# Giving the matmuls of a gathered row tile in one block: layers 2 and 3 of a graph attention kernel

## The chip, the cores and the metric

The kernel runs on one core of a Trainium2 chip. The metric is the device time of one execution in microseconds; the time given for a kernel is the median of several executions. Beside the times there is one execution with a profile, which shows the work of each engine: PE (matmuls) with PEld (its weight loads), DVE, ACT and POOL (elementwise work; POOL here issues the indirect gathers), and SP, which issues plain DMAs.

## The reference

Four graph attention layers over N = 4096 nodes with 256 features and one adjacency matrix, of which about 0.4% of the entries (and the diagonal) are set. Each layer is wrapped in a residual and a layer norm:

```python
x = _layernorm(x + _L0_gnn_ref(x, adj, ...))   # 4 heads of 64
x = _layernorm(x + _L1_gnn_ref(x, adj, ...))   # 4 heads of 64
x = _layernorm(x + _L2_gnn_ref(x, adj, ...))   # 2 heads of 128
x = _layernorm(x + _L3_gnn_ref(x, adj, ...))   # softmax and negative softmax, fc, elu
```

Layers 2 and 3, which the change touches, come down to this:

```python
# layer 2: two heads
e = leaky_relu(s1[:, None, :] + s2[None, :, :], 0.2)
att = softmax(where(adj[:, :, None] == 1, e, NEG), axis=1)
h_prime = einsum('ijh,jhc->ihc', att, W3h)

# layer 3: one logit, two softmaxes over the same neighbours
e = leaky_relu(Wh1 + Wh2.T, 0.2)
attention = softmax(where(adj > 0, e, NEG_INF), axis=1)
negative_attention = -softmax(where(adj > 0, -e, NEG_INF), axis=1)
h_prime_double = concatenate([attention @ x, negative_attention @ x], axis=1)
return elu(h_prime_double @ fc_W)
```

## The kernel before, in words

The 4096 nodes are 32 tiles of 128 rows. Since the adjacency is sparse, most tiles of a layer are *gathered*: for the 128 target rows of a tile the value rows of their neighbours are fetched by indirect DMA into slots of 128 rows, weights are worked out for each slot, and matmuls with the weights as the stationary operand and the fetched rows as the moving one sum them up. A bit mask per slot says which target row each fetched row belongs to.

A row tile has two halves of seven slots. A slot is used in one of two ways. A *full* slot has a 128x128 weight tile and gives one matmul. A slot of a *pair* holds neighbours of only 64 of the target rows; it has a 128x64 weight tile, and the two slots of a pair write to the two halves of the output's partitions. Half 0 has the tile's own rows as its full slot (fetched by a plain DMA that SP issues in `load`, line 797) and three pairs, so six gathers; half 1 has two pairs and three full slots, so seven gathers. `FULL` and `PAIRS` (lines 80 and 81) list the places; `parts` (line 807) gives each its slots. The gathers are issued by POOL at line 802.

For each half, `half` (line 840) makes the mask (`unpack`), then the weights `w`: in layer 2 by exponentials on ACT (line 912) and a masking step on DVE (line 914), in layer 3 by ACT at lines 879, 880 and 882 and by DVE at 881 and 883. Behind these stand the matmuls (line 933), once for each of the two heads (layer 2) or of the two softmaxes (layer 3). In layer 2 the row has 2 x 129 columns and both heads share a bank; in layer 3 each softmax has 257 columns and a bank of its own. Each matmul in the source gives two records in the profile.

The order of the matmuls at line 933 in layers 2 and 3 is set by the loop over `turns`. With F for full and P for pairs, and the heads in turn, layer 2 gives F P, P F in half 0 and F P, P F in half 1; layer 3 gives F P, F P in half 0 and F P, P F in half 1. The last half of the last tile of layer 3 has a function of its own, `last_half`, which gives each place as soon as its weights are there.

Some tiles are not gathered but *whole*: `whole_rows` (line 1173) goes through all 32 column tiles for four or three target tiles at once. It fetches values (`vw`, through SP's queue, four ahead), makes dense weights (`pw`, ACT and DVE, lines 1205 and 1206 in layer 2, 1208 to 1213 in layer 3) and multiplies (line 1216). Layer 2 has 11 whole and 21 gathered tiles, layer 3 seven and 25. This work is cut into units, and `whole` gives some of them after each half, so that they spread evenly over the gathered tiles.

`steps` runs `part(m, 0)` and `part(m, 1)` for each gathered tile, and `half_with_whole` gives, for each part, this order of work: loads and gathers of tiles `m` and `m + 1` (in part 0), the transposes of a projection for the next layer if one is ready (line 682), the half itself, the copy of the transposed tile (`xT`, ACT, line 687) and the projection's matmuls (line 696), the end of the tile before, units of whole tiles, and the projection's values. A projection is the matmul of a finished row tile with the next layer's weights; layer 3 has none. At a layer's end, `close` gives half 0 of the next layer's tiles 0 and 1 ahead of time.

This is an order of priority; a scheduler in the framework moves instructions on each engine where that lets them start sooner, and puts in the waits. Each engine then works in its own fixed order.

Buffers come from pools. `wp` has five buffers for `w`, each half taking one. `g0` and `g1` have four slots each for the gathered rows of half 0 and half 1; a slot holds all seven rows of a half in layer 2, and four of them in layer 3 (`PER`), where a half thus takes two slots. `ld` has four buffers for the target rows' logits, `vp` six for `vw` and `dp` eight for `pw`. A buffer comes free with the last instruction that reads it, so a gather waits until the matmuls of an earlier tile have read its slot.

Of the kernel before, what the change touches and what calls it, by code (L numbers as in the profile page):

```python
# [50 lines left out]
P = 128  # L51
# [27 lines left out]
UNITS = (1 + FIRST, NPACK - FIRST)  # L79
FULL = ((0,), tuple(range(NPAIR - FIRST, NPACK - FIRST)))  # L80
PAIRS = (tuple(range(1, 1 + FIRST)), tuple(range(NPAIR - FIRST)))
# [8 lines left out]
HEADS = (4, 4, 2, 2)  # L90
WIDTH = (65, 65, 129, 257)
# [670 lines left out]
class RowTile:  # L762
# [3 lines left out]
    def __init__(self, layer, step, m):  # L766
        self.layer, self.step, self.m = layer, step, m
        self.slots = {}
        self.accs = None

    def slot(self, half, s):
        L, n = self.layer, self.layer.n
# [64 lines left out]
        u, k = FULL[half][0], 0 if own else two  # L837
        spread(L.nc, words[:, u:u + len(FULL[half]), :], bits[:, k:k + len(FULL[half])], pat)

    def half(self, half):  # L840
        L, n, nc = self.layer, self.layer.n, self.layer.nc
        prog, sh, S = L.prog, L.shared, self.S
        H, Wd, V, T, A = HEADS[n], WIDTH[n], VALS[n], TERMS[n], LOGS[n]
        if self.accs is None:
            pool = prog.ptwo[1 if n == 3 and self.step % 2 else 0]
            self.accs = [prog.bank(pool) for _ in range(2 if n == 3 else 1)]
        accs, U = self.accs, UNITS[half]
        parts = self.parts(half)
        if n < 2:

# [4 lines left out]
            mh = there.bitcast(U8)  # L855
            mh2 = mh.rearrange("p (o i) -> p o i", o=1).to_broadcast([P, 2, U * P])
        else:
            there = prog.mkp.tile([P, UNITS[1], P // 4], I32, name="mk")[:, :U]
            self.unpack(half, there)
            mh = there.rearrange("p t i -> p (t i)").bitcast(U8).rearrange("p (t i) -> p t i", t=U)  # L860
        pairs = [prog.wp.tile([P, 2, UNITS[1], P], F32, name="w") for _ in range(H // 2)]
        w = [pair[:, k, :U] for pair in pairs for k in range(2)]
        if n < 2:
            w = [w[1], w[2], w[3], w[0]]
# [8 lines left out]

        if n == 3:
            if half == 1 and self.step == L.count - 1:
                return self.last_half(accs, parts, w, mh)
            for u in range(U):
                for rows, g in parts[u]:
                    nc.scalar.activation(w[0][:, u, rows], S[:, 0, rows], AF.Relu, bias=d(g, 0))  # L879
# [1 line left out]
            nc.vector.tensor_tensor(w[1], w[1], mh, op=ALU.mult)  # L881
            self.exps = nc.scalar.activation(w[0], w[0], AF.Exp, bias=sh["shift2"])
            nc.vector.tensor_tensor(w[0], w[0], mh, op=ALU.mult)
            turns = ((1,), (0,))
        else:
            for h in range(A, T):
                dd = self.slot(half, 0)[:, :HALF * ROW[n]].rearrange("p (t c) -> p t c", t=HALF)
                k = 0
                for us in sorted((PAIRS[half], FULL[half])):
                    two = us == PAIRS[half]  # L890
                    a, b = us[0], us[-1] + 1
                    e = (2 if two else 1) * (b - a)
                    rows = P // (e // (b - a))
# [23 lines left out]
            if n == 0:  # L917
                with self.layer.prog.tc.issue_after(last.ins):
                    nc.vector.tensor_scalar(self.kept(half), self.came(half), 0, None, op0=ALU.bitwise_or)
            turns = ((3, 0), (1, 2)) if n < 2 else ((0,), (1,))  # L920


        for t, heads in enumerate(turns):
            for us in (FULL[half], PAIRS[half])[::-1 if t == 1 and (half == 1 or n < 3) else 1]:
                for h in heads:
                    for u in us:
                        for rows, g in parts[u]:
                            a = accs[h][rows, :Wd] if n == 3 else accs[0][rows, h * Wd:(h + 1) * Wd]
                            b = g[:, h * Wd:(h + 1) * Wd]
                            if n < 2:  # L930
                                a = accs[0][rows, h * Wd:(H + 1) * Wd].rearrange("p (s c) -> p s c", c=Wd)[:, ::H - h]
                                b = b.rearrange("p (s c) -> p s c", s=1).to_broadcast([P, 2, Wd])
                            nc.tensor.matmul(a, w[h][:, u, rows], b,  # L933
                                             start=half == 0 and u == 0 and (n == 3 or h == turns[0][0]),
                                             stop=half == 1, skip_group_check=True)

    def last_half(self, accs, parts, w, mh):

# [21 lines left out]
class Layer:  # L960
# [62 lines left out]
    def half_alone(self, m, part):  # L1023


        self.step = 2 * m + part
        proj, middle = None, self.middle
        second = m > NT - (LATE if self.n == 0 else 6) and len(self.ready) > 1
        if self.ready and self.ready[0][0] < self.step and (part == 0 or second):
            self.set_banks()  # L1030
            if part == 1 and self.n == 0:
                self.prog.banks = self.prog.pplace
            proj = Projection(self.prog, self.n + 1, self.nxt, *self.ready.pop(0)[1:])
            proj.transpose()
        if part == 1 or self.tile(m).accs is None:
            self.tile(m).half(part)
        for p in self.stored:
            p.store()
        if proj is not None:
            proj.copy()  # L1040
        if proj is not None:
            proj.multiply()
        if middle is not None:
            middle.values()
        if part == 1 and m >= 1:
            self.tile(m - 1).finish()
        if middle is not None:
            middle.edge()
        self.stored, self.middle = [middle] if middle is not None else [], proj

    def half_with_whole(self, m, part):
# [12 lines left out]
        with ExitStack() as order:  # L1064
            for ins in self.last:
                order.enter_context(self.prog.tc.issue_after(ins))
            self.last = ()
            if part == 1 or self.tile(m).accs is None:
                self.tile(m).half(part)
                if self.outs:  # L1070


                    order.enter_context(self.prog.tc.issue_after(self.tile(m).exps.ins))
                    self.store_rows()
# [777 lines left out]
```

## Time and profile before

| | us |
|---|---|
| time, median of 3 executions (2794.93 to 2804.66) | 2798.34 |
| the profiled execution, its own time | 2791.46 |
| span of the profile | 2789.7 |
| PE busy | 2102.6 |
| DVE busy | 1550.7 |
| ACT busy | 1508.9 |
| POOL busy | 1392.2 |
| gathers on POOL (line 802), 1378 | 1386.9 |
| gathered matmuls (line 933), 9268 records, all layers | 1164.6 |
| whole-tile matmuls (line 1216), 2304 records | 415.1 |
| projections (line 696), 640 records | 214.1 |

The span is the time from the first to the last instruction of the profiled execution. Busy times of PE count a pipelined matmul with its modelled end, so the mean of one record is longer than the distance from one record's start to the next. Layer 2 runs from about 1770 to 2250 us in the span, layer 3 from about 2274 on.

### The profile page before, as it was taken

What the parts mean: (1) busy time and instruction counts of PE and PEld (TensorE: products, weight loads), DVE (VectorE), ACT (ScalarE), POOL (GpSimd) and SP (SyncE); (2) the same over time, 40 slices, a digit from 0 to 9 for tenths busy, and PEclk for the clock granted to TensorE, in tenths of its full rate; (3) what the DMA queues carried; (4) which work ended last, traced back from release to release, by engine and by line L of the source; (5) the groups of instructions that cost most, each with busy time, mean ns of one, the idle gap of its engine ahead of it and who ended that gap; (6) DMA issues with size and microseconds to landing.
All of it is one profiled execution on the core that took longest, in us unless ns stands there. A gap on an engine that the chain in (4) does not pass through costs nothing.

```text
span 2789.7 us, 46645 instructions
## 1 busy us (share of the span) xinstructions
PE 2102.6 (75%) x15137; PEld 1662.9 (60%) x15137; DVE 1550.7 (56%) x5130; ACT 1508.9 (54%) x4705; POOL 1392.2 (50%) x1413
## 2 busy tenths in 40 slices
PE   5546677667676675688787888768888889988886
PEld 3335555455455564567666676657877766765654
DVE  3335545455454355556565656647756656666565
ACT  5446455455454354444454545456756647766663
POOL 0254534434435444555555553456656446666663
PEclk7667777677676688788888888879989999999988
DMA  8767565555553344344444444335556567878774
GB/s 278 249 202 222 163 176 164 163 163 175 156 148 111 86 121 137 109 134 125 127 122 128 124 118 120 110 107 162 166 147 172 150 190 226 243 240 249 241 231 129
DMA packets 294057, 459.20 MB, mean 165 GB/s; under 512 B 90982, under 2 KB 206795, under 8 KB 293804
## 3 DMA queue, kind: packets, MB, share of 16 engines
q0 software_dynamic: 76544, 233.01, 29.2%
q1 hardware_dynamic: 212642, 218.92, 26.2%
q10 hardware_dynamic: 4618, 4.20, 0.4%
q8 instruction: 122, 2.00, 0.3%
q14 instruction: 131, 1.07, 0.1%
HBM read 407.14 MB, written 48.81 MB: 163 GB/s over the span
## 4 chain that ended last, share of the span: by engine, by line
PE 49%; issue 13%; ACT 4%; POOL 3%; DMA 2%; DVE 2%; another core or an unknown queue 1%; SPq 0%; ACTq 0%; POOLq 0%; DVEq 0%
PE bank L933 26%; PE bank L1216 12%; PE bank L696 4%; ACT w L912 3%; POOL G L802 3%; PE bank L1279 2%; PE bank L1277 2%; DMA G<-vals,idx 1%; PE bank L682 1%; PE bank L699 1%; DVE w L869 0%; ACT pw L1205 0%; PE bank L527 0%; PE bank L529 0%
## 5 line engine op out<-in xcount | busy, mean ns | idle before, releaser
L802 POOL DMA_INDIRECT G<-vals,idx x1378 | 1386.9, 1006 | 1365.2 <-issue 651.9
L933 PE MATMUL bank<-G,w 128*64 128x130 f32 (+5 forms) x9268 | 1164.6, 329 | 393.7 <-issue 357.6
L933 PEld LDWEIGHTS bank<-G,w 128*64 128x64 f32 (+1 forms) x9268 | 895.4, 173 | 632.1 <-issue 526.3
L912 ACT ACTIVATE w<-S,G 128x64 f32<-128x64 f32 (+1 forms) x3108 | 827.1, 350 | 104.5 <-issue 24.8
L1216 PE MATMUL bank<-vw,pw 128*128 128x129 f32 (+1 forms) x2304 | 415.1, 333 | 77.1 <-issue 72.8
L1216 PEld LDWEIGHTS bank<-vw,pw 128*128 128x128 f32 x2304 | 357.5, 203 | 130.2 <-issue 100.6
L869 DVE SCALAR_TENSOR_TENSOR w<-w,bank 128x1024 f32<-128x1024 f32 (+1 forms) x240 | 322.8, 1345 | 116.9 <-ACT w L912 103.0
L696 PE MATMUL bank<-wext,xT 128*128 128x268 f32 (+3 forms) x640 | 214.1, 472 | 38.8 <-ACT xT L687 24.5
L716 ACT ACTIVATE row<-bank 128x4 f32<-128x4 f32 (+1 forms) x128 | 21.6, 169 | 322.2 <-remote 106.6
L1205 ACT ACTIVATE pw<-Sw,d 128x512 f32<-128x512 f32 (+1 forms) x192 | 128.3, 679 | 119.9 <-remote 58.7
L1206 DVE SCALAR_TENSOR_TENSOR pw<-pw,mw 128x512 f32<-128x512 f32 (+1 forms) x192 | 122.1, 643 | 114.8 <-ACT pw L1205 86.6
L696 PEld LDWEIGHTS bank<-wext,xT 128*128 128x128 f32 x640 | 135.7, 231 | 74.8 <-ACT xT L687 27.9
L879 ACT ACTIVATE w<-S,G 128x64 f32<-128x64 f32 (+1 forms) x343 | 111.3, 354 | 101.3 <-DMA G<-vals,idx 58.4
L687 ACT COPY xT<-bank 128x256 f32<-128x256 f32 x128 | 46.3, 364 | 210.2 <-PE bank L682 132.8
L718 DVE COPY row<-bank 128x6 f32<-128x6 f32 (+2 forms) x128 | 20.0, 156 | 229.9 <-ACT row L716 202.3
L404 ACT ACTIVATE mk<-raw 128x1024 uint8<-128x1024 int32 x128 | 129.1, 1049 | 18.2 <-DMA raw<-in_adjB_dram 8.3
L1279 PE MATMUL bank<-pw,vw 128*65 128x128 f32 x512 | 115.7, 313 | 2.5 <-issue 2.4
L1213 DVE TENSOR_TENSOR pw<-pw,mw 128x512 f32<-128x512 f32 (+1 forms) x128 | 79.1, 621 | 68.7 <-ACT w L879 12.4
L1277 PE MATMUL bank<-vw,pw 128*128 128x65 f32 x512 | 102.9, 288 | 15.9 <-issue 15.7
L1277 PEld LDWEIGHTS bank<-vw,pw 128*128 128x128 f32 x512 | 94.5, 230 | 28.3 <-issue 26.9
L747 ACT ACTIVATE erow<-bank,shift 4x128 f32<-4x128 f32 (+1 forms) x96 | 33.5, 352 | 130.9 <-PE bank L737 77.9
L515 DVE TENSOR_TENSOR under<-bank,ranks 128x512 f16<-128x512 f32 x32 | 21.9, 685 | 139.9 <-remote 68.4
(197 smaller groups left out, 2179.6 us busy)
## 6 DMA issues: line engine op xcount, KB each, us to landing
raw<-in_adjB_dram SPq DMA_DIRECT2D x128, 512.0 KB
G<-vals,idx POOLq DMA_INDIRECT x1378
vw<-vals SPq DMA_DIRECT2D x128, 128.5 KB
S<-edge SPq DMA_DIRECT2D x60, 256.0 KB
vw<-vals SPq DMA_DIRECT2D x96, 129.0 KB
xp<-y SPq DMA_DIRECT2D x96, 128.0 KB
y<-xp SPq DMA_DIRECT2D x96, 128.0 KB
vals<-row SPq DMA_DIRECT2D x64, 152.0 KB
```

What stands on the lines that cost most here:

```text
L404: nc.scalar.activation(self.mk[:, 2 * q:2 * q + 2], src, AF.Copy)
L696: nc.tensor.matmul(pp[:, :c1 - c0], self.xT[:, k, :], wext[:, k, c0:c1], start=(k == 0), stop=(k == KT - 1 and brow is None))
L802: nc.gpsimd.indirect_dma_start(out=self.row(half, k), out_offset=None, in_=self.values[:N + 1 if half else MIX * P, :].rearrange("r (k c) ...
L869: return nc.vector.scalar_tensor_tensor(pair, pair, LEAST, mh2, op0=ALU.max, op1=ALU.mult)
L879: nc.scalar.activation(w[0][:, u, rows], S[:, 0, rows], AF.Relu, bias=d(g, 0))
L912: nc.scalar.activation(w[h][:, u, rows], S[:, h, rows], AF.Exp, bias=d(g, h))
L933: nc.tensor.matmul(a, w[h][:, u, rows], b, start=half == 0 and u == 0 and (n == 3 or h == turns[0][0]), stop=half == 1, skip_group_check=True)
L1205: nc.scalar.activation(p, S[:, h, :g], AF.Exp, bias=d)
L1206: nc.vector.scalar_tensor_tensor(p, p, LEAST, mj, op0=ALU.max, op1=ALU.mult)
L1216: nc.tensor.matmul(accs[it][:, c:c + Wd], p[:, it, :], v[:, c:c + Wd], start=(j == 0 and h == heads[0]), stop=(j == NT - 1), skip_group_ch ...
L1277: nc.tensor.matmul(bu[:, it * Wd:(it + 1) * Wd], p[up][:, it, :], v[:, up * Wd:(up + 1) * Wd], start=j == 0 and it == 0, **how)
L1279: nc.tensor.matmul(bf[:Wd, it * P:(it + 1) * P], v[:, flat * Wd:(flat + 1) * Wd], p[flat][:, it, :], start=j == 0 and it == 0, **how)
```

## The change

In layers 2 and 3, `half` for part 0 makes its mask and weights as before but gives no matmuls: it puts the half on a list (`held`). Part 1 makes its own weights, and then `multiply_held` gives the matmuls of both halves in one block: the full slot of half 0 (the tile's own rows), the pairs of half 0, the pairs of half 1, and the full slots of half 1, each for both heads or softmaxes. The output banks are taken at the first matmul. Layers 0 and 1 keep their order of matmuls, through the same new function `multiply`. The halves that `close` gives ahead of time are not held. In the last half of layer 3's last tile the held half is given in front of `last_half`.

```diff
-    def half(self, half):
+    def half(self, half, hold=False):
+        self.begun = True
...
-        if self.accs is None:
-            pool = prog.ptwo[1 if n == 3 and self.step % 2 else 0]
-            self.accs = [prog.bank(pool) for _ in range(2 if n == 3 else 1)]
-        accs, U = self.accs, UNITS[half]
+        U = UNITS[half]
...
             if half == 1 and self.step == L.count - 1:
-                return self.last_half(accs, parts, w, mh)
+                self.multiply_held()
+                return self.last_half(self.accs, parts, w, mh)
...
-            turns = ((1,), (0,))
...
-            turns = ((3, 0), (1, 2)) if n < 2 else ((0,), (1,))
-        for t, heads in enumerate(turns):
-            for us in (FULL[half], PAIRS[half])[::-1 if t == 1 and (half == 1 or n < 3) else 1]:
-                for h in heads:
-                    for u in us:
-                        for rows, g in parts[u]:
...
-                            nc.tensor.matmul(a, w[h][:, u, rows], b,
-                                             start=half == 0 and u == 0 and (n == 3 or h == turns[0][0]),
-                                             stop=half == 1, skip_group_check=True)
+            turns = ((0,), (1,)) if n == 2 else ((0, 1), (2, 3)) if A == T else ((3, 0), (1, 2))
+        if n < 2:
+            for t, heads in enumerate(turns):
+                for us in (FULL[half], PAIRS[half])[::-1 if t == 1 else 1]:
+                    for h in heads:
+                        self.multiply(half, h, us, parts, w, h == turns[0][0])
+            return
+        self.held.append((half, parts, w))
+        if not hold:
+            self.multiply_held()
+
+    def multiply(self, half, h, us, parts, w, first):
+        n = self.layer.n
+        H, Wd = HEADS[n], WIDTH[n]
+        if self.accs is None:
+            pool = self.layer.prog.ptwo[1 if n == 3 and self.step % 2 else 0]
+            self.accs = [self.layer.prog.bank(pool) for _ in range(2 if n == 3 else 1)]
+        accs = self.accs
+        for u in us:
+            for rows, g in parts[u]:
+                a = accs[h][rows, :Wd] if n == 3 else accs[0][rows, h * Wd:(h + 1) * Wd]
+                b = g[:, h * Wd:(h + 1) * Wd]
...
+                self.layer.nc.tensor.matmul(a, w[h][:, u, rows], b, start=half == 0 and u == 0 and first,
+                                            stop=half == 1, skip_group_check=True)
+
+    def multiply_held(self):
+
+        n, held = self.layer.n, self.held
+        heads = (0, 1) if n == 2 else (1, 0)
+        for group in (FULL, PAIRS):
+            for half, parts, w in held:
+                if half == 0:
+                    for h in heads:
+                        self.multiply(half, h, group[half], parts, w, n == 3 or h == heads[0])
+        for group in (PAIRS, FULL):
+            for half, parts, w in held:
+                if half == 1:
+                    for h in heads:
+                        self.multiply(half, h, group[half], parts, w, False)
+        self.held = []
...
-            if part == 1 or self.tile(m).accs is None:
-                self.tile(m).half(part)
+            if part == 1 or not self.tile(m).begun:
+                self.tile(m).half(part, hold=part == 0 and self.n > 1)
```

More of the change, by code (lines that the diff above doesn't have):

```diff
@@ L769, in __init__ @@
         self.accs = None
+        self.begun = False
+        self.held = []
     def slot(self, half, s):
@@ L919, in half @@
                     nc.vector.tensor_scalar(self.kept(half), self.came(half), 0, None, op0=ALU.bitwise_or)
-            turns = ((3, 0), (1, 2)) if n < 2 else ((0,), (1,))
-        for t, heads in enumerate(turns):
-            for us in (FULL[half], PAIRS[half])[::-1 if t == 1 and (half == 1 or n < 3) else 1]:
-                for h in heads:
-                    for u in us:
-                        for rows, g in parts[u]:
[L928 to L933, printed above, removed]
-                                             start=half == 0 and u == 0 and (n == 3 or h == turns[0][0]),
-                                             stop=half == 1, skip_group_check=True)
+            turns = ((0,), (1,)) if n == 2 else ((0, 1), (2, 3)) if A == T else ((3, 0), (1, 2))
@@ new lines, in half @@
+        if n < 2:
[18 more added lines that the diff above has]
+                b = g[:, h * Wd:(h + 1) * Wd]
+                if n < 2:
+                    a = accs[0][rows, h * Wd:(H + 1) * Wd].rearrange("p (s c) -> p s c", c=Wd)[:, ::H - h]
+                    b = b.rearrange("p (s c) -> p s c", s=1).to_broadcast([P, 2, Wd])
+                self.layer.nc.tensor.matmul(a, w[h][:, u, rows], b, start=half == 0 and u == 0 and first,
+                                            stop=half == 1, skip_group_check=True)
@@ new lines, in multiply_held @@
+    def multiply_held(self):
[11 more added lines that the diff above has]
+                        self.multiply(half, h, group[half], parts, w, False)
+        self.held = []
@@ L1067, in half_with_whole @@
             self.last = ()
-            if part == 1 or self.tile(m).accs is None:
-                self.tile(m).half(part)
+            if part == 1 or not self.tile(m).begun:
+                self.tile(m).half(part, hold=part == 0 and self.n > 1)
                 if self.outs:
```

## The prediction

> **What bounds the kernel now.** I read the page's totals, then the chain of work that ended last, then the stretches by stage, then the timeline of one row tile in each of the two layers that change.
>
> ```profile
> span 2789.7 us, 46645 instructions
> PE 2102.6 (75%) x15137; PEld 1662.9 (60%) x15137; DVE 1550.7 (56%) x5130; ACT 1508.9 (54%) x4705; POOL 1392.2 (50%) x1413
> PE 49%; issue 13%; ACT 4%; POOL 3%; DMA 2%; DVE 2%; another core or an unknown queue 1%; SPq 0%; ACTq 0%; POOLq 0%; DVEq 0%
> 1840.00:2240.00 400.00, 341.84 (x2594) 297.31 (x2593) 271.99 (x960) 267.66 (x800) 230.05 (x215) 0.91 0.56 155
> 2300.00:2700.00 400.00, 358.67 (x1826) 255.47 (x1826) 258.01 (x965) 271.86 (x631) 264.92 (x259) 0.94 0.78 239
> ```
>
> In the stretches the columns are length, PE, PEld, DVE, ACT, POOL, granted clock, DMA share, GB/s. Half of the last chain is PE. In the steady part of layer 2 (1840 to 2240) PE is busy for 342 of 400 us, in layer 3 (2300 to 2700) for 359 of 400; no other engine is over 272. So matmul time saved in these stretches counts, as long as nothing else comes up. Next, how gathered matmuls run (layer 3, then layer 2):
>
> ```profile
> 2412.11 0.41 PEld L933 LDWEIGHTS bank<-G,w 128*128 128x128 f32 x2
> 2412.32 4.13 PE L933 MATMUL bank<-G,w 128*128 128x257 f32 x28
> 2412.84 1.06 PEld L933 LDWEIGHTS bank<-G,w 128*64 128x64 f32 x12 [0.33 <-issue]
> 2414.30 0.30 PEld L933 LDWEIGHTS bank<-G,w 128*128 128x128 f32 x2 [0.39 <-issue]
> 2414.93 1.06 PEld L933 LDWEIGHTS bank<-G,w 128*64 128x64 f32 x12 [0.33 <-issue]
> 2416.38 3.73 PE L1216 MATMUL bank<-vw,pw 128*128 128x257 f32 x16
> 2419.95 4.85 PE L933 MATMUL bank<-G,w 128*128 128x257 f32 x28
> 2005.93 2.28 PE L933 MATMUL bank<-G,w 128*128 128x129 f32 x28
> 2008.41 0.37 ACT L687 COPY xT<-bank 128x256 f32<-128x256 f32 x1 [0.55 <-PE bank L933]
> 2008.83 2.01 PE L696 MATMUL bank<-wext,xT 128*128 128x256 f32 x8 [0.62 <-issue]
> ```
>
> Wherever a batch changes between 128- and 64-column weights, the weight loads pause by 0.33 or 0.39 us. Successive records of layer 3 start 0.217 us apart for a whole tile and as a pair of 64-column records (0.112 us in layer 2). Half 0 of layer 3 has 4 whole records and 24 of 64 columns, 16 such places: 16 x 0.217 = 3.47 us. It takes 2412.32 to 2416.38 = 4.06, 0.59 more, with two round trips into pairs and back. Half 1 has 12 whole and 16 of 64, 20 places = 4.34 us; it takes 2419.95 to 2424.63 = 4.68, 0.34 more, with one. In layer 2 half 0 takes 2.12 against 16 x 0.112 = 1.79, 0.33 more, with one. So a round trip costs about 0.30 us in both layers.
>
> **The change part by part.** No instruction is added or removed; PE's get another order, and half 0's are moved from part 0 to part 1.
>
> Layer 3 removes two of three round trips per tile: 2 x 0.30 x 24 tiles (the last one keeps its own order in half 1) = 14.5 us. Layer 2 removes one of two: 0.30 x 21 = 6.3 us. Both lie on the engine that sets the end: 20.8 us gross.
>
> What is moved: half 0's matmuls (4.1 us in layer 3, 2.3 in layer 2) go behind the whole-tile matmuls of part 0, which move forward by as much. Five things hang on this.
>
> (1) Gather slots. In layer 3 a half has two slots per tile out of four, so the six half-0 gathers of tile k wait for half 0 of tile k-2; SP's load of its own rows waits for the same, in front of the vw loads that follow it in SP's queue. Now the release comes inside the block: that starts the moved 4.1 us before the old start of half 1, and its half-0 part takes about 3.5, so about 0.6 us before that old start. (Layer 2 has one slot per half and tile, four tiles ahead: no wait.) The tiles whose gather starts too early for that, by the listed starts of gathers and matmuls: tile 8's gather starts 2421.33, half 1 of tile 6 at 2419.95, no delay; tile 10's starts 2460.96, but half 1 of tile 8 only at 2466.3, so 4.7 us late. Over all tiles I sum about 33 us of such delays, the longest 6.5. The release of half 1's slots comes 1 to 2 us earlier, since the block ends earlier.
>
> ```profile
> 2441.27 0.94 POOL L802 DMA_INDIRECT G<-vals,idx  x1 [1.72 <-ACT w L879]
> 2460.96 0.94 POOL L802 DMA_INDIRECT G<-vals,idx  x1 [2.53 <-ACT pw L1208]
> ACT w L879 <- DMA G<-vals,idx: 32.6, 38, 1.9
> ACT w L879 <- DMA G<-vals: 13.1, 6, 4.6
> ```
>
> The first two are the starts of half 0 of tiles 9 and 10 on POOL, 19.7 us apart; the last two are waits of ACT (us, times, longest) for gathered and own rows. A tile's 13 gathers took 2279.9 to 2298.1 = 18.2 us where POOL ran unhindered; in the steady stretch it is 19.7. So POOL can make up 1.5 us per tile, 36 us over 24 tiles, about as much as the delays. The last gather of a half 1 is issued 19 to 29 us before its matmuls, and needs some 8.5 (landing 3 to 5, ACT and DVE about 4.5), so single delays of 5 are covered. Without cover, a late gather holds ACT, which works in order, and behind it the pw weights of whole tiles, which PE then waits for. Ends: 0 and 33 us; I take 4, since lead and spare both cover the sum.
>
> (2) SP's wait: four vw tiles are fetched ahead of PE at that point, about 5 to 7 us of PE work, against six before. If the own-row load waits under 5 us, no vw is late. I take 0; uncovered it is the same few us per tile as in (1), and is in its upper end.
>
> (3) w buffers: five, two per tile. Half 0's w is now held until the block (longer by the whole-tile work between the halves), half 1's is freed as before. ACT has the weights of half 0 ready 10 to 20 us before use, so three free buffers still hold a tile and a half. I take 0; its failure would look like (1).
>
> (4) Layer 2: xT. Transposes of a projection stand ahead of a half, and PE multiplies the result (L696) behind it. Part 0 had 2.3 us of half 0 between them, and ACT saw the transposes 2.3 to 2.8 us after their start (2005.72 to 2008.41). Now only three to five whole-tile matmuls stand there, 0.7 to 1.1 us; part 1 has 4.4 us instead of 2.7.
>
> ```profile
> PE bank L696 <- ACT xT L687: 8.6, 10, 2.3
> PE bank L696 <- issue: 8.1, 11, 1.6
> ```
>
> Of these 16.7 us in 21 waits I put about half, 8, into part 1, where they should go. In part 0, about 15 projections wait between 0 and 1.5 us longer; no row shows the short cover, so the bounds are 0 and 23 us, and nearest is the row above (0.62 us with a cover of 2.3): 0.9 each, 13. Net +5 (ends -8 and +15).
>
> Here a rule of the Trainium skill speaks against the change. The longest PE waits in these rows are 2.3 us (for xT) and 2.4 (layer 3, before L1216), with a granted clock of 0.91 and 0.94. "TensorE: Matmul & The Clock Gate", section "HAM oscillation — how this bites in real kernels", says that a PE pause over some 3.4 us makes the clock fall back, and then at least a short stretch[...] is run at half speed. A 2.3 us wait for xT that loses 1.5 us of cover would reach 3.8. By the trace, waits below that cost only themselves: +5. By the rule, if each of about 15 part-0 projections passed the limit, 15 x 1.7 = 26 us more (an estimate from that page). Since 20 of the 21 waits are shorter by the rows' means (0.8 us), I take the trace, and leave the rule to the upper end.
>
> (5) The seam of layers 2 and 3: half 0 of the last layer 2 tile (2.3 us, at 2229.7) waited beside other work and now is behind. PE idles 7 us there at 2268 for xT, so at most 2.5 is lost; I take 1. Tiles 0 and 1 of layer 3 give half 0 at once, as before.
>
> Sum: -14.5 - 6.3 + 4 + 0 + 0 + 5 + 1 = -10.8 us. The profiled execution took 2791.46 us (span 2789.7 and 1.8 around it): 2780.7. It stands 6.9 below the median of 2798.34, so against the median: 2787.5.
>
> **The rivals.** *No change.* PE's saved time turns into waits, since other streams set the beat.
>
> ```profile
> PE bank L1216 <- issue: 30.5, 29, 2.4
> PE bank L933 <- issue: 6.9, 8, 1.8
> ```
>
> PE in layer 3 stands 30.5 us ahead of L1216 without a named releaser, most behind a batch, and POOL's 18.2 us per tile is close under the period of 19.7. For it: a tile can gain at most 1.5 us, and 0.6 is asked. Against: PE is at 90%. If layer 3 gives nothing and layer 2 only its 6.3 less 5 and 1, the time is 2798; with half of layer 3, 2791. Span of this case 2790 to 2803.
>
> *Slower.* Item (1) prevails: half-0 gathers chained to the block. It decides when POOL loses more than its spare 1.5 us per tile, that is when the mean delay (33/24 = 1.4 us by the starts of before) exceeds it, as it can because a later gather makes the next block later too. At a period longer by 1 us for 23 tiles, and layer 2 as summed (0): 2791.5 + 23 = 2814 on the profiled scale, 2821 by the median; at 0.5 us, 2810. For it: the delays and the spare are of one size, and ACT already waits 46 us for gathers. Against: gathers lead their matmuls by 19 us or more.
>
> *It does not do what it says.* The order on PE could have been broken up by the scheduler. The instruction order of the changed kernel shows 128-, 64-, then 128-column matmuls once per tile, so I give this nothing.
>
> **How the numbers follow.** Forecast (faster, about 2775 to 2790): 0.47. No change: 0.22. Slower: 0.31. About 0.3% is what a measurement of this kernel can tell from no change, 8.4 us: faster ends at 2789.9, slower begins at 2806.7; each case lies within its limits but for its edge. Forecast's own range: 2770 (item 4 at its lower end, item 1 at 0: -20.8 - 8 + 1 = -27.8) to 2792. For 8 in 10 I go from 2770 to 2815: left out are the larger periods of the slower case, about 0.12, and less than 0.05 below.
>
> **What would show it.** Right: in layer 3 a block of 56 records in about 8.1 us (36 x 0.217 + 0.3) instead of 4.1 and 4.8; in layer 2 about 4.4 instead of 2.3 and 2.7; the starts of half-0 gathers under 19.5 us apart; ACT's wait for gathers still about 46 us. Wrong by (1): POOL's first half-0 gather waits for the gathered matmuls over 3 us in most tiles, periods over 20 us, ACT's waits for gathers doubled, and PE's before L1216 naming pw. Wrong by (4): L696 waiting over 25 us in layer 2, and a granted clock under 0.9. A layer 3 with period 19.7 and more PE waits by "issue" would show the no-change case.

## The result: 3.9% slower

| | before | changed |
|---|---|---|
| median of 4 executions, us | 2796.64 | 2910.27 |
| ratio, 95% interval | | 1.0385 (1.0316 to 1.0455) |
| span of the profile, us | 2789.7 | 2912.7 |
| layer 2, us | 485 | 568 |
| layer 3, us | 538 | 570 |

The layers are read from the profiled executions: layer 2 from the last gathered matmul of layer 1 to its own last one, layer 3 from there to the end. Both became longer, layer 2 by 83 us and layer 3 by 32. (The other 8 us of the difference between the two profiled executions lie in layers 0 and 1, which the change leaves alone.) The time lies outside the forecast range of 2770 to 2815 us, and far above the 2821 us of the prediction's slower case.

The page's head and the stretches of the changed kernel (columns as above):

```profile
span 2912.7 us, 46636 instructions
PE 2125.6 (73%) x15137; PEld 1710.1 (59%) x15137; DVE 1540.7 (53%) x5130; ACT 1506.2 (52%) x4705; POOL 1378.2 (47%) x1413
1840.00:2240.00 400.00, 282.85 (x2083) 251.61 (x2080) 217.22 (x745) 215.65 (x639) 182.75 (x179) 0.80 0.45 124
2300.00:2700.00 400.00, 345.97 (x1838) 270.19 (x1839) 238.90 (x935) 245.20 (x585) 217.73 (x211) 0.91 0.70 209
```

In 400 us of layer 2 PE starts 2083 records instead of 2594, and every other engine is less busy as well: nothing became the bound by having more to do.

The blocks themselves are as the change meant them. Timeline, one block of layer 3 and one of layer 2:

```profile
2479.48 8.31 PE L945 MATMUL bank<-G,w 128*128 128x257 f32 x56
2480.44 4.10 PEld L945 LDWEIGHTS bank<-G,w 128*64 128x64 f32 x40 [0.33 <-issue]
2484.92 2.46 PEld L945 LDWEIGHTS bank<-G,w 128*128 128x128 f32 x12 [0.39 <-issue]
2026.13 4.50 PE L945 MATMUL bank<-G,w 128*128 128x129 f32 x56
```

One pause into the pairs, one out. 8.31 us stand against 4.13 and 4.85 before, 4.50 against 2.28 and 2.73. So the loss is around the blocks. From the timeline of layer 2 behind a block that ended at 1999.5 (rows between are left out):

```profile
2004.75 0.38 PE L682 MATMUL bank<-ident,y 128*128 128x128 f32 x2
2004.97 0.58 PE L1243 MATMUL bank<-vw,pw 128*128 128x129 f32 x3
2005.90 0.27 PE L1243 MATMUL bank<-vw,pw 128*128 128x129 f32 x1 [0.35 <-issue]
2006.60 0.72 ACT L1232 ACTIVATE pw<-Sw,d 128x512 f32<-128x512 f32 x1 [2.76 <-PE bank L682]
2006.62 0.46 PE L1243 MATMUL bank<-vw,pw 128*128 128x129 f32 x2 [0.45 <-issue]
2010.91 0.72 ACT L1232 ACTIVATE pw<-Sw,d 128x512 f32<-128x512 f32 x1 [3.11 <-remote]
2012.15 1.02 POOL L804 DMA_INDIRECT G<-vals,idx  x1 [0.30 <-issue]
2013.48 0.94 POOL L804 DMA_INDIRECT G<-vals,idx  x1 [0.30 <-issue]
2016.60 0.72 ACT L1232 ACTIVATE pw<-Sw,d 128x512 f32<-128x512 f32 x1 [4.73 <-remote]
2017.77 0.34 ACT L687 COPY xT<-bank 128x256 f32<-128x256 f32 x1
2018.17 3.81 PE L696 MATMUL bank<-wext,xT 128*128 128x256 f32 x8 [11.09 <-ACT xT L687]
```

POOL gives 13 gathers in a row from 1997.8 to 2014.4, one every 1.25 to 1.45 us. PE's records come to a halt at 2007.1, where the next matmuls need xT. ACT stands three times in front of a `pw`, and xT, which is behind these on ACT, comes 12.6 us after the end of the transposes. The releasers shown are no help here ("remote"). In the program's order each of these ACT instructions waits only for a matmul that has read the buffer before, and by its record that matmul had ended 4.5, 7.9 and 12.7 us earlier. The semaphore events of PE (the signals by which it tells that a matmul is done) say the same: they come at 2006.58, 2010.89 and 2016.58, each 0.02 us before ACT starts.

So I matched, in both traces, every wait of ACT and DVE whose last missing signal was PE's (idle over 0.2 us) with the end of the record that the program makes it wait for; the time between that end and the start of the waiting instruction is how late the signal was:

| signal | before, layer 2 | changed, layer 2 | changed, layer 3 |
|---|---|---|---|
| PE to ACT, median (largest) us | 2.31 (11.2) of 73 | 3.00 (13.6) of 62 | 5.96 (16.0) of 15 |
| ACT to DVE, median us | 0.03 | 0.03 | 0.03 |

Only PE's results are late, and the kernel before had this too: I had not seen it, since a row's "end" for PE is modelled. Without gathers in the last 9 us the same wait takes 0.04 to 0.09 us. Next I cut a steady part of layer 2 (1840 to 2210 before, 1840 to 2290 changed) into quarters of a us by the number of gathers begun 2 to 12 us earlier, and counted PE's work as records started times their undisturbed distance (0.112 us a full record, half for a pair's, 0.22 for a projection's):

| gathers begun 2 to 12 us ago | before: us, work per us | changed: us, work per us |
|---|---|---|
| 0 to 2 | 12, 1.00 | 119, 0.94 |
| 4 to 6 | 269, 0.70 | 140, 0.54 |
| 7 | 74, 0.53 | 76, 0.21 |
| 8 | 7, 0.15 | 81, 0.09 |

At full density of gathers (eight in 10 us) PE all but stands. The kernel before had it for 7 us of 370, the changed one for 81 of 450; over the whole of layer 2 it is about 36 and 111 us, again some 75 us more. That is where the time went; the experiments ask why, and whether it is the cause. The number of gathers alone does not set PE's pace: with seven of them the work is 0.53 in one kernel and 0.21 in the other.

### The profile page after: what moved, and what is told of

Same layout as the page of the kernel before. It is cut to its first block, busy times and chain, and to the rows that moved or that the text cites. A ratio compares the mean times of both kernels' runs of the same rounds, so it can differ in the third digit from the quotient of the medians.

```text
span 2912.7 us, 46636 instructions
## 1 busy us (share of the span) xinstructions
PE 2125.6 (73%) x15137; PEld 1710.1 (59%) x15137; DVE 1540.7 (53%) x5130; ACT 1506.2 (52%) x4705; POOL 1378.2 (47%) x1413
## 5 line engine op out<-in xcount | busy, mean ns | idle before, releaser
L804 POOL DMA_INDIRECT G<-vals,idx x1378 | 1372.8, 996 | 1502.2 <-issue 667.6
L945 PE MATMUL bank<-G,w 128*64 128x130 f32 (+5 forms) x9268 | 1179.4, 335 | 455.9 <-issue 412.8
L945 PEld LDWEIGHTS bank<-G,w 128*64 128x64 f32 (+1 forms) x9268 | 933.1, 176 | 680.3 <-issue 579.2
L1243 PEld LDWEIGHTS bank<-vw,pw 128*128 128x128 f32 x2304 | 364.3, 205 | 111.4 <-issue 82.6
L696 PE MATMUL bank<-wext,xT 128*128 128x268 f32 (+3 forms) x640 | 214.3, 475 | 83.2 <-ACT xT L687 78.7
L1232 ACT ACTIVATE pw<-Sw,d 128x512 f32<-128x512 f32 (+1 forms) x192 | 128.3, 679 | 201.8 <-remote 125.1
L696 PEld LDWEIGHTS bank<-wext,xT 128*128 128x128 f32 x640 | 137.5, 233 | 118.3 <-ACT xT L687 83.9
L1304 PEld LDWEIGHTS bank<-vw,pw 128*128 128x128 f32 x512 | 94.4, 229 | 29.5 <-issue 27.8
L1235 ACT ACTIVATE pw<-Sw,d 128x512 f32<-128x512 f32 (+1 forms) x128 | 83.1, 656 | 55.0 <-remote 33.3
```

What stands on the lines that cost most here:

```text
L696: nc.tensor.matmul(pp[:, :c1 - c0], self.xT[:, k, :], wext[:, k, c0:c1], start=(k == 0), stop=(k == KT - 1 and brow is None))
L804: nc.gpsimd.indirect_dma_start(out=self.row(half, k), out_offset=None, in_=self.values[:N + 1 if half else MIX * P, :].rearrange("r (k c) ...
L945: self.layer.nc.tensor.matmul(a, w[h][:, u, rows], b, start=half == 0 and u == 0 and first, stop=half == 1, skip_group_check=True)
L1232: nc.scalar.activation(p, S[:, h, :g], AF.Exp, bias=d)
L1243: nc.tensor.matmul(accs[it][:, c:c + Wd], p[:, it, :], v[:, c:c + Wd], start=(j == 0 and h == heads[0]), stop=(j == NT - 1), skip_group_ch ...
L1304: nc.tensor.matmul(bu[:, it * Wd:(it + 1) * Wd], p[up][:, it, :], v[:, up * Wd:(up + 1) * Wd], start=j == 0 and it == 0, **how)
```

## The experiments

The kernel before took 2761 to 2811 us beside five sets of runs and 2011 and 2016 us beside two, by the chip that they ran on. Each chip was used for one set, so the runs do not tell a property of a chip from a state that it was in at that time. Ratios are to the kernel before on the same chip. I name the chips by what they show: late (PE's results come late) and prompt (0.04 to 0.09 us in every matched wait of layers 2 and 3). The recorded profiles of before and changed are of the late kind. The kinds differ most in layers 0 and 1, which end at 1138 to 1145 us on prompt chips and at 1723 to 1784 on late ones where their gathers are as before.

**Where: one layer at a time.** Edit, for layer 3 and for layer 2:

```diff
-                self.tile(m).half(part, hold=part == 0 and self.n > 1)
+                self.tile(m).half(part, hold=part == 0 and self.n == 3)   # or == 2
```

> Half 0 is held in layer 3 alone; layer 2 has its old order. Late-signal theory (in layers 2 and 3 what PE finishes reaches ACT, DVE and SP late while gathers are in flight, and the move puts the gathers in one unbroken burst behind the block, so that PE waits for its own results): layer 2 ends at about 2251 us as before, layer 3 is longer by about 31 us (570 against 538): time about 2828, 2815 to 2840. Gather-release theory (late half-0 slots hold ACT in layer 3, as the prediction's slower case has it): layer 3 alone carries the loss, so well above 2850. Clock theory (PE pauses over 3.4 us lower the granted clock): those pauses are in layer 2, so layer 3 is no longer than before: 2785 to 2798.

> Half 0 is held in layer 2 alone; layer 3 has its old order. Late-signal theory: layer 2 ends at about 2343 us instead of 2251, layer 3 as before at 538: time about 2885, 2870 to 2895; PE's waits for xT before the projection stay near 50 us per 400. Gather-release theory of layer 3: no loss here, 2790 to 2800. Clock theory: the whole loss, about 2905.

Late chip. Layer 3 alone: 1.0085 (1.0040 to 1.0129), 2789.87 against 2764.35. Layer 2 alone: 1.0251 (1.0212 to 1.0289), 2826.94. Layer 3 takes 567 us where it is held and 533 where not; layer 2 544 and 481. That is 26 us where I expected 31, and 63 where I expected 85 to 90; the sum, 1.034, is about the change's. Neither rival fits, since the loss is in both layers and most of it in layer 2. (The clock theory is the Trainium skill's rule that the prediction names.)

**Order alone, nothing moved.** In the kernel before:

```diff
-            turns = ((1,), (0,))
+            turns = ((1, 0),)
...
-            turns = ((3, 0), (1, 2)) if n < 2 else ((0,), (1,))
+            turns = ((3, 0), (1, 2)) if n < 2 else ((0, 1),)
```

with full then pairs in half 0, pairs then full in half 1.

> The order inside each half alone is changed and nothing is moved between the parts: half 0 gives full then pairs for both heads, half 1 pairs then full. Layer 3 has two round trips into pairs per tile instead of three, layer 2 still two. Switch theory of the prediction: 0.30 us x 24 = 7.2 us less, about 2789. If the order of matmuls itself, not the move, were what costs: slower than 2797, by some part of the 114 us.

Late chip: 0.9979 (0.9958 to 1.0001), 2758.21 against 2764.35. The 6 us have the expected size, but the interval reaches 1. The order is not what costs.

**Is the wait for xT the cause?** In part 0 of the changed kernel:

```diff
         for proj in projs:
             proj.copy()
-            proj.multiply()
...
         self.whole(2 * m + part)
+        for proj in projs:
+            proj.multiply()
```

> As the changed kernel, but in part 0 the projection's matmuls stand behind the whole-tile units instead of in front of them, so that some 16 to 24 whole-tile matmuls (3.6 us and more) lie between the transposes and the matmuls that need xT. Late-signal theory: the wait for xT in layer 2 (about 11 us each, mostly in part 0) shrinks by the about 2.9 us of cover gained, some 19 times, so 40 to 60 us less than the changed kernel: about 2860; most of the wait stays, since the transposes' end still reaches ACT only when the gathers are over. Clock theory: shorter pauses, but still over 3.4 us, so no more than the same. Gather-release theory: no change, about 2910.

Late chip: 1.0397 (1.0348 to 1.0446), 2866.52 us, no better than the change, whose ratio is 1.031 to 1.039 in four sets (on this chip it was not run). Waits of PE in layer 2 (1840 to 2240; us, times, longest), of the changed kernel, then of this one:

```profile
PE bank L696 <- ACT xT L687: 52.1, 8, 11.1
PE bank L1243 <- issue: 48.1, 68, 4.4
```

```profile
PE bank L1247 <- issue: 67.5, 107, 1.7
PE bank L1247 <- remote: 9.7, 1, 9.7
```

The wait for xT is gone, and 29 us more than in the changed kernel are now lost in front of whole-tile matmuls, most of them by "issue", with no releaser named. The rest went into longer records: PE is busy for 309 of 400 us instead of 283, for nearly as many records (2134 and 2083). So the xT wait was a place, not the cause; I had expected 40 to 60 us from it. This run does not settle what the clock is worth: in layer 2 one pause of PE over 3.4 us is left instead of eight, but the granted clock hardly rose (0.82 against 0.80 in 1840 to 2240; at half for 205 us of layer 2 instead of 225).

**Are gathers the cause?** In layers 2 and 3 every gather becomes a plain DMA of 128 consecutive rows of the same size, issued by POOL at the same place:

```diff
+            if n >= 2:
+                j = (m + k) % MIX
+                nc.gpsimd.dma_start(out=self.row(half, k), in_=self.values[j * P:(j + 1) * P, :ROW[n]])
+                continue
```

> The changed kernel with plain DMAs of consecutive rows in place of the gathers of layers 2 and 3 (sums over other rows), again, for a chip on which PE's results come late. Late-signal theory: with the gathers gone from layers 2 and 3 the late signals and PE's stalls there go with them, so that there the time is far below the kernel before (by 250 us or more, since PE's stalls and waits for its own results are some 100 us in each of the two layers). If any dense stream of transfers from POOL holds PE, these at 0.53 us apart hold it more than gathers at 1.25: no faster than the changed kernel. On a chip where results come at once: 0.96 of the kernel before, as in the first such run.

Late chip: 0.9118 (0.9092 to 0.9144), 2516.02 us; the changed kernel itself took 2867.6 on that chip. The stretches of layers 2 and 3:

```profile
1790.00:2060.00 270.00, 261.56 (x2356) 243.46 (x2354) 235.91 (x902) 232.00 (x715) 110.27 (x209) 0.99 0.78 237
2140.00:2440.00 300.00, 284.13 (x1597) 219.11 (x1597) 208.48 (x844) 217.40 (x532) 118.70 (x224) 0.96 0.82 275
```

PE is busy 97 and 95% of the time, and all 20 matched waits for PE in these stretches take 0.04 us (in the changed kernel up to 16). Layer 2 takes 333 us and layer 3 454. The whole time is 245 us below the kernel before, about the 250 expected. In these stretches the core's transfers move more per us than with gathers (237 GB/s against 124), and the plain ones follow each other at 0.53 us: it is neither bytes nor transfers from POOL in close sequence as such. What holds PE comes with the indirect gather. The run does not tell its parts apart: the index per row, the scattered rows that it reads (the plain DMA reads consecutive ones), and POOL's longer work on each (about 1 us).

On a prompt chip the same pair:

> The changed kernel, but in layers 2 and 3 each gather is a plain DMA of as many consecutive rows, issued by POOL at the same place; the rows are not the neighbours' (the sums over gathered rows are of other rows). If it is the indirect form (an index per row) that holds PE, the loss of the change is gone: within 1% of the plain form of the kernel before. If it is any transfer of that size that POOL issues in close sequence, the plain form of the change is still 3 to 4% over the plain form of before.

> The kernel before with the same replacement of gathers by plain DMAs of consecutive rows in layers 2 and 3 (the sums over gathered rows are of other rows). If the indirect form holds PE: PE's stalls in layer 2 (82 of 395 us) mostly go, 30 to 60 us less than before. If it is any such transfer: within 1% of before.

0.9586 (0.9554 to 0.9618) and 0.9563 (0.9533 to 0.9594), 1929.7 and 1923.0 us. Layer 2 takes 335 and 337 us, as on the late chip: without gathers the two kinds of chip are alike there. (The plain form of the kernel before was run on a prompt chip only.) The two forms are within 1% of each other, as expected; the plain form of before gains 88 us where 30 to 60 were expected. This pair is also the best test of the saved switches, since PE is busy for 98% of layer 2 and 95% of layer 3 in the plain form of before. PE's busy time falls by 3 us in layer 2 and 9 in layer 3 (the prediction has 6.3 and 14.5), but the change gains nothing: by the medians it is 7 us slower. Layer 3 takes 457 us against 445 in the profiled executions, of which that of the changed form was its slowest (1939.0); why is open.

**Is it their closeness?** The change puts 13 gathers in a row where there were bursts of six and seven with pauses. Three small memsets behind every gather of layers 2 and 3 space them, without another byte moved from memory; the next gather of the half is kept behind them:

```diff
+            for _ in range(3 if n >= 2 else 0):
+                with prog.tc.issue_after(got.ins):
+                    got = nc.gpsimd.memset(sh["pause"], 0.0)
```

First on a prompt chip:

> The changed kernel with three small memsets on POOL (about 0.1 us each) behind every gather of layers 2 and 3, so that gathers are issued about 1.6 us apart instead of 1.25. Density theory (PE all but stands while gathers follow each other without a pause: in the changed kernel's layer 2 it does 0.97 us of work per us with up to two gathers begun 2 to 12 us ago, 0.1 to 0.2 with eight; spread out, as in the kernel before with six, 0.7): layer 2 gets shorter although its gathers take 4 to 5 us longer per tile, from 31 us per tile to 25 or less, so 80 us or more less there; layer 3 within 20 us of the changed kernel; time 0.98 to 1.02 of the kernel before. Release theory (the block frees all gather slots at once, and POOL's 16.5 us of gathers behind it are the path): each tile is longer by 4 to 5 us, 45 tiles, so 1.08 or more.

> The kernel before with the same memsets behind every gather of layers 2 and 3. There the gathers are already spread (13 in about 20 us); 13 at 1.6 us are 21 us and more than the 19.7 of layer 3's period. Density theory: PE is a little faster in layer 2, POOL becomes the bound in layer 3: 1.00 to 1.03 of the kernel before. Release theory: POOL is longer by 4 us per tile where it has 1.5 to spare: 1.03 to 1.06.

1.0978 (1.0944 to 1.1013) and 1.1063 (1.1028 to 1.1099): where nothing is late, only POOL's longer time is seen. The density theory's numbers failed here; the release theory's held for the changed kernel (1.08 or more), not for the kernel before (1.03 to 1.06). Then on a late chip, beside the change:

> The changed kernel with three small memsets on POOL behind every gather of layers 2 and 3 (gathers 1.54 us apart instead of 1.25), again, for a chip on which PE's results come late. Density theory: 13 gathers take 20 us instead of 16.5, but PE works beside them at 0.6 of its speed instead of 0.15: layer 2 at 22 to 25 us per tile instead of 29 to 31, so 100 us or more less than the changed kernel there, and 0.98 to 1.02 of the kernel before. Release theory (the gathers behind the block are the path as such): 3.5 us more per tile, 45 tiles, so 1.09 of the kernel before. On a chip without late results: 1.10, as it was there.

> The kernel before with the same memsets, for a chip on which PE's results come late. Density theory: layer 2 gains what PE stands beside gathers at 1.25 us (some 80 us of stalls in 400) less what POOL becomes longer; layer 3 is bound by POOL at 13 x 1.54 + 2 = 22 us: 0.98 to 1.03. Release theory: 1.04 to 1.11, as on the chip without late results.

> The changed kernel beside the three others on the same chip: 1.03 to 1.04 of the kernel before where PE's results come late (before at about 2760 to 2800), 0.99 to 1.02 where they do not (before at about 2010).

| late chip, same set | median us | ratio to before | layer 2 | layer 3 |
|---|---|---|---|---|
| changed | 2851.97 | 1.0306 (1.0230 to 1.0383) | 539 | 562 |
| changed, spaced | 2795.12 | 1.0111 (1.0057 to 1.0164) | 472 | 593 |
| before, spaced | 2812.77 | 1.0187 (1.0136 to 1.0239) | 468 | 606 |

More work on POOL makes the changed kernel 57 us faster. Layer 2 is 67 us shorter (100 or more were expected); layer 3, where POOL is busy for 373 of 470 us (2230 to 2700), pays 31 back. Layer 2 now takes as long as on the prompt chip, 472 us in both spaced runs of the change. Waits of PE in layer 2 (1800 to 2180), changed, then changed and spaced, and under these the longest wait of ACT in the spaced kernel:

```profile
PE bank L696 <- ACT xT L687: 47.1, 6, 10.4
PE bank L1243 <- issue: 44.3, 49, 3.1
```

```profile
PE bank L697 <- ACT xT L688: 55.7, 9, 15.0
PE bank L738 <- DVE row L731: 26.4, 9, 8.8
PE bank L1253 <- issue: 2.6, 2, 2.4
ACT w L922 <- DMA G<-vals,idx: 87.5, 59, 5.5
```

The stalls without a named releaser are gone. PE still waits for xT, but for another reason: ACT, which works in order, now waits 87.5 us for gathers, as POOL has become slower.

In the same stretch PE starts 2306 records instead of 2008, though POOL is busy for 308 us instead of 190:

```profile
1800.00:2180.00 380.00, 262.56 (x2008) 237.36 (x2007) 208.46 (x718) 207.34 (x610) 190.38 (x185) 0.82 0.47 131
```

```profile
1800.00:2180.00 380.00, 283.77 (x2306) 259.55 (x2305) 236.99 (x859) 238.58 (x719) 307.93 (x878) 0.85 0.56 156
```

ACT's matched waits for PE have a median of 0.04 us (18, the largest 3.1). So, on this chip and in layer 2, the closeness decides: at 1.25 us apart PE's results pile up, at 1.54 hardly. A prompt chip shows the other side: in layer 2 of the order-only kernel (run e10_paced01_1, gathers 1.25 us apart) PE does 0.75 us of work per us with eight gathers begun 2 to 12 us ago, where the changed kernel did 0.09 on a late one. And with the gathers spaced the change is no longer worse: 2795 against 2813 here, 2208 against 2227 on the prompt chip, with ranges that do not meet. In layer 3 it is 13 and 20 us shorter.

**Moved, in the old order.** In `multiply_held`:

```diff
-        for group in (FULL, PAIRS):
...
+        for half, parts, w in held:
+            for t, h in enumerate(heads):
+                for group in (FULL, PAIRS)[::-1 if t == 1 and (half == 1 or n < 3) else 1]:
+                    self.multiply(half, h, group[half], parts, w, n == 3 or h == heads[0])
```

> The changed kernel with half 0 moved into part 1, but the matmuls of each half in the order of the kernel before (layer 2: full, pairs, pairs, full in each half; layer 3: full, pairs, full, pairs and full, pairs, pairs, full). Switch theory: slower than the changed kernel by what the switches cost, 21 us. If PE stands for the gathers anyway and its own time does not count there: within 5 us of the changed kernel in layer 2's share (6 us), and most of layer 3's share (14.5 us) kept.

Late chip, same set: 1.0439 (1.0380 to 1.0497), 2878.58 against the change's 2851.97. The 27 us are of the size of the switch term (21): the four executions took 2864 to 2890 us, three of the change's 2837 to 2855 and one 2882. But they lie elsewhere: in the profiled executions layer 2 is longer by 17 us and layer 3 by 9, where the term has 6.3 and 14.5. So the size alone does not confirm it.

**The change once more.**

> The changed kernel again, since the kernel before took 2764 us beside one set of experiments and 2011 us beside another: on some chips what PE finishes reaches the other engines at once (0.04 us), on others up to 13 us late while gathers are in flight. Late-signal theory: where the kernel before takes about 2770 to 2800, the change is again 3 to 5% slower; where it takes about 2010, the change loses little, and the switches saved (21 us) are set against the gathers' later release: 0.98 to 1.02. Release theory: the loss is the same everywhere, about 110 us.

> The changed kernel once more. On a chip without late results (kernel before at about 2015): the saved switches (21 us) against later gather releases in layer 3 and POOL's 16.5 us of gathers behind each block of layer 2: 0.99 to 1.02. The release theory's full loss (110 us) would be 1.055. On a chip with late results: 1.03 to 1.04, as before.

1.0342 (1.0265 to 1.0419) and 1.0358 (1.0302 to 1.0414), both on late chips. On a prompt chip the change as it is was never run; whether it gains there is open.

**A version that beats both on a late chip.** If close gathers hold PE in layer 2, they should in layers 0 and 1, which have as many per tile. The same memsets there, and only there, on the order-only kernel:

```diff
+            for _ in range(3 if n < 2 else 0):   # or 1
+                with prog.tc.issue_after(got.ins):
+                    got = nc.gpsimd.memset(sh["pause"], 0.0)
```

> The order-only kernel (nothing moved between the parts) with three small memsets on POOL behind every gather of layers 0 and 1, so that these are 1.54 us apart instead of 1.25. Density theory, on a chip on which PE's results come late (kernel before at about 2765): PE no longer stands beside the gathers, and layers 0 and 1 become bound by POOL: 780 gathers x 1.54 = 1200 us and about 150 before them, so they end at 1350 to 1500 instead of 1740, and the time is 2400 to 2550, 0.87 to 0.92. Release theory, or if spacing helps in layer 2 for a reason of its own: layers 0 and 1 are no shorter, 1.00 or more. On a chip without late results: 1.05 to 1.10, since POOL is the bound there already.

> The same with one memset behind each gather of layers 0 and 1, 1.33 us apart. Density theory: the effect is steep (0.2 of PE's speed at eight gathers in 10 us, 0.7 at six), so at seven and a half part of the gain: between the kernel before and the kernel with three memsets, 0.93 to 0.98. On a chip without late results: 1.02 to 1.03.

> The order-only kernel with gathers of layers 0 and 1 spaced to 1.54 us. Density theory, on a chip with late results: layers 0 and 1 end at 1350 to 1500 us instead of 1740, time 0.87 to 0.92 of before. On a chip without: 1.13, as measured.

The first two fell on a prompt chip: 1.1286 (1.1255 to 1.1317) and 1.0114 (1.0084 to 1.0145), both outside what was expected there (1.05 to 1.10 and 1.02 to 1.03); one memset on a late chip was not run. On a late chip, three memsets: 0.8769 (0.8724 to 0.8814), 2463.21 us against 2810.54. Layers 0 and 1 end at 1434 us there, and at 1784 in the changed kernel of the same set. Its page:

```profile
span 2459.3 us, 48845 instructions
PE 1984.2 (81%) x15137; PEld 1595.9 (65%) x15137; DVE 1548.8 (63%) x5130; ACT 1512.7 (62%) x4705; POOL 1676.5 (68%) x3753
```

So the largest gain of this study, 12%, lies outside the changed layers, is idle work on one engine (the order alone gave 0.2%), and was seen on one late chip; on a prompt one it is a loss of 13%.

## Why the prediction was wrong

*The switches.* The blocks take 8.31 and 4.50 us, as foreseen (8.1 and about 4.4), so the cost of a switch was read rightly. What was wrong is what this time was worth: PE was taken for the bound of layers 2 and 3 by its busy share, while part of that was PE standing beside gathers (0.70 us of work per us with four to six of them). That 20.8 us could be had is not shown: order alone gave 6 of 7.2 us with an interval that reaches 1, the plain pair gave nothing, and the spaced pair's 18 to 19 us come in kernels in which POOL's time counts.

*Item (1), gather slots.* The step that failed is the sentence in brackets, "Layer 2 has one slot per half and tile, four tiles ahead: no wait." POOL runs ahead until the slots are used up, so it waits for the release however many there are; it did so in the kernel before. Waits of POOL in layer 2 (1840 to 2240), before and changed:

```profile
POOL G L802 <- ACT w L912: 23.7, 9, 9.1
POOL G L802 <- PE bank L933: 22.8, 3, 17.2
```

```profile
POOL G L804 <- ACT w L912: 93.0, 7, 16.6
POOL G L804 <- PE bank L945: 31.1, 3, 16.9
```

The rows put most of these waits down to ACT; by the program each is for a gathered matmul, and in the changed kernel the first gather of a burst starts 0.3 to 0.8 us behind the record of that matmul in nearly every case. Before, half 0's slots came free in part 0 and half 1's in part 1; now the block frees both, POOL waits 9 to 17 us for it in most tiles, and then gives 13 gathers in a row. Against the 0 us that item (1) has for layer 2 stand 83 us, and 63 us in the run that holds layer 2 alone. For layer 3 I priced only the delay, and took 4 us against 32 measured. The delay did come:

```profile
2547.63 1.05 POOL L804 DMA_INDIRECT G<-vals,idx  x1 [4.76 <-ACT w L880]
2568.84 1.60 POOL L804 DMA_INDIRECT G<-vals,idx  x1 [4.61 <-ACT w L881]
```

21.2 us between half 0 of tiles 9 and 10 (before 19.7), with all 13 gathers of tile 9 in between without a pause. ACT's waits for gathered and own rows grew as the slower rival said, from 45.7 to 68.4 us, by half and not to double:

```profile
ACT w L880 <- DMA G<-vals,idx: 48.1, 46, 7.7
ACT w L880 <- DMA G<-vals: 20.3, 6, 4.7
```

That rival had the place right and its price for layer 3 (half to one us per tile: 12 to 23 us; measured 32) roughly right, but not the whole mechanism, and no price for layer 2. That late slots alone explain layer 3 is not shown either: PE's signals are late there too (median 5.96 us).

*Item (4), xT.* The place was named, and both its signs of being wrong came true: waits of 52.1 us for xT before L696 (over 25), a granted clock of 0.80 (under 0.9). The size was not: 0.9 us more per wait in part 0, against 6.5 on average and up to 11.1, from 0.9 before. Nor was the cause, since taking these waits away gained nothing. I read the 2.3 to 2.8 us from transposes to ACT as a fixed latency that a cover hides. They were a sample of PE's lateness, which grows with the gathers in flight, and the row with them was in front of me.

*The clock.* Behind the pause that began at 2007.1 the granted clock is at half from 2010.5, 3.4 us later, to 2024.1. There the trace agrees with the rule that the prediction took from the Trainium skill ("TensorE: Matmul & The Clock Gate", section "HAM oscillation — how this bites in real kernels": no pauses of PE over about 3.4 us). Elsewhere PE's records do not show it: in the kernel before, the clock is at half 13 times between 1840 and 2240, with no pause over 2.3 us. So the prediction's "waits below that cost only themselves" is not what the trace shows. The estimate of 26 us was off too: about 1.7 us is, on that page, the time run at half speed, of which half is lost, so 13 us. What it cost can be estimated from the traces, as half of PE's busy time at half clock: in layer 2, 40 us before and 55 changed; in layer 3, 27 and 43. That is some 15 us of the 83, and some 16 of the 32, of which I took none. No run changed the clock alone.

*Items (2), (3), (5).* Nothing in the runs points to them; none was tested by itself.

*Settled and open.* Shown on late chips: the loss needs the indirect gathers (plain DMAs take it away) and, in layer 2, their closeness (spacing takes it away there). That closeness acts in layer 3 is not shown, since spacing makes POOL too slow there. Only in the traces: that PE's finished work becomes known late. Open: what in an indirect gather does that, why some chips do not have it, and whether PE computes late or only reports late. Two things speak for computing late: PE's own records leave gaps (0.35 and 0.45 us at 2005.9 and 2006.6 above) for which the profile names no wait, and the clock falls where the records show no long pause, as it would by the page's rule if PE stood idle there. For reporting late speaks that at the end of the burst four completions come within 0.17 us (2016.58 to 2016.75), for over 1 us of matmul work.

## What to carry to other kernels

A change of order on one engine also changes when buffers come free, and so the rhythm of the engine that fills them: ask whether two releases that were apart become one, and what a burst does to the others. Before a busy engine is called the bound, look at how late its results reach those who wait for them, by the program's waits and not by the releasers shown, and split that by what else is in flight. A remedy found in this way is to be run on more than one chip.

## What was not expected of the hardware

- With unbroken runs of indirect gathers from POOL 1.25 us apart (seven or eight begun 2 to 12 us ago), PE did 0.1 to 0.2 us of work per us in the changed kernel's layer 2, and its results reached ACT up to 14 us late there and 16 in layer 3; at 1.54 us apart the median in layer 2 was 0.04 us. Plain DMAs of as many consecutive rows, 0.53 us apart, did nothing of the kind.
- This was seen on some chips only, each used once. The same kernel took 2761 to 2811 us on those and 2011 to 2016 on the others.
- Three memsets on POOL behind each gather of layers 0 and 1 made a kernel 12% faster on one chip of the first kind and 13% slower on one of the second.
